# A fused graph network on one core: the mix product in three narrow passes, and gate products joined into three operations per half of the features

## The chip, the cores and the metric

The kernel runs on one core of a Trainium2 chip. The metric is the device time of one execution in microseconds (us), as the median of several runs. A core has five engines that run side by side, each with its own queue in a fixed order: TensorE (PE, the matmuls; PEld is its loading of the stationary operand), VectorE (DVE), ScalarE (ACT), GpSimd (POOL) and SyncE (SP, which here only starts DMA transfers). They wait for one another through semaphores. Matmuls accumulate into PSUM, which here is eight banks of 128 partitions x 512 float32 values; all else lies in SBUF.

## The reference, cut to what matters

64 graphs of 256 nodes with 256 features pass through two layers. The first is a gated network of three steps, each of which multiplies the features by a weight, sums them over the neighbours and updates the state with a gated recurrent cell. The second is an attention layer whose softmax weights, `alpha`, mix the projected features.

```python
def _gru_cell(inp, h, w_ih, w_hh, b_ih, b_hh):
    gi = inp @ w_ih.T + b_ih
    gh = h @ w_hh.T + b_hh
    i_r, i_z, i_n = jnp.split(gi, 3, axis=-1)
    h_r, h_z, h_n = jnp.split(gh, 3, axis=-1)
    r = jax.nn.sigmoid(i_r + h_r)
    z = jax.nn.sigmoid(i_z + h_z)
    n = jnp.tanh(i_n + r * h_n)
    return (1.0 - z) * n + z * h
...
for i in range(L):
    m = jnp.einsum('bnd,de->bne', h, weight[i])
    aggr = jnp.einsum('bst,bsd->btd', A, m)
    h = _gru_cell(aggr, h, w_ih, w_hh, b_ih, b_hh)
...
h = jnp.einsum('bnd,od->bno', x, W)
e = (h @ a_left)[:, :, None] + (h @ a_right)[:, None, :]
e = jnp.where(e > 0, e, LEAKY_SLOPE * e)
e = jnp.where(adj_matrix == 0, NEG_INF, e)
alpha = jax.nn.softmax(e, axis=-1)
return jnp.einsum('bij,bjd->bid', alpha, h)
...
h = jnp.maximum(_layernorm(x, axis=-1), 0.0)
x = x + _L0_gnn_ref(h, adj, ...)
h = jnp.maximum(_layernorm(x, axis=-1), 0.0)
x = x + _L1_gnn_ref(h, adj, ...)
```

## The kernel before, in words

**Tiling.** Two graphs form a pair, and there are 32 pairs (`NPAIR`). The state of a pair is kept transposed: two tiles `hT[db]`, one for each half of the features (`db` = 0, 1), of 128 features x 512 columns, which are the 256 nodes of both graphs. The weight of a step and the input weight of the cell are multiplied into one matrix in the set-up, so a step is a product with the adjacency (`prop`, L802) and the products of the gates (L665).

**Products in narrow passes.** Most products are not done in float32. Each operand is held three times: rounded to float32r (class `round`), the remainder of that in float16, and the value itself scaled down in float16 (class `half`). A product of two such operands is one float32r pass and two float16 passes that add into the same bank; for the weights the three parts are `fac` and the two planes of `low`. `split16` makes the three parts of an activation: `rounded` on ScalarE (L616), `remainder` on VectorE (L620 or L622), `whole_of` on ScalarE from PSUM (L627) or on VectorE from SBUF (L629). `limbs` does the first two for `prop` (L651, L652). Three products stay in float32: the turns by TensorE, the work of the last two pairs' attention, and `mix` (L953).

**Gates.** `gate` takes one bank and records one or two TensorE operations on it. For each half of the features there are five operations: r from the state (`topT`), r from the neighbours (`topF`), nh from the state, ni from the neighbours, and z from both. Each of these terms is six matmuls with 512 columns: two float32r and four float16. An operation that is `mixed` begins with the type that the operation before it ended with (`narrow`), so it holds one change of type. From the banks, ScalarE makes r (L820) and z (L833) and adds a bias to nh (L687); VectorE makes u = (r + 1) nh (L825) and adds ni (L828); ScalarE takes the tanh (L830); VectorE updates `hT[db]` with d sub, d mul and d add (L837, L839, L841).

**Attention.** Normalised features `hb[g]` of graph `g` (L738), the scores, mask and exponentials (L896, L922, L925, L927, L933) give `pm_[g]`. It is turned by a DMA transpose and two gathers, and a ScalarE copy (`join`, L710) puts the halves of each number together in `pT`. Then `mix` multiplies `hb[g]` by `pT`: four float32 matmuls with 256 columns, for each graph of a pair. Its bank is split (`c`) and multiplied by W (`project`, L964: four float32r and eight float16 matmuls of 256 columns), and L980 adds the result to the output rows. The last two pairs (`p >= NPAIR - 2`) copy the bank instead and project in float32 (L971, L975), and the last pair works in smaller pieces (L998 to L1014).

**Order.** No loop sets the order. Every operation is recorded with an engine, a cost in ns (`n`), a latency, its reads and writes and a due time, and `Plan.run` lists them: again and again it takes, over all engines, the operation that can start first by these costs; ties go by priority, which is the due time less the latency of what follows, less a hand-set number of the table `LEAD` (by name, with the prefix "first", "late" or "last" for pairs 0, 30 and 31). Operations of up to four pairs (`WINDOW`) are open at once. Buffers come from fixed sets: 28 `full`, 22 `round`, 40 `half`, 8 `bank`. The list fixes each engine's queue; on the chip the engines then only wait for semaphores. `dve2` marks VectorE operations that the plan keeps apart from GpSimd's.

Of the kernel before, what the change touches and what calls it, by code (L numbers as in the profile page):

```python
# [10 lines left out]
F32 = mybir.dt.float32  # L11
# [19 lines left out]
    "A": -111500, "A16": -23000, "G": -500, "b_nh": -3500, "b_rz": 1000, "b_rz half": 7500, "back 0": 27500,  # L31
    "back 0 gather": 88000, "back 0 of 0": 32000, "back 0 of 1": 18000, "back 1": 28500, "back 1 gather": -33000,
    "back 1 of 0": -500, "back 1 of 1": 20500, "back copy 0": -80500, "back copy 1": -5000, "c0 0": -2500,
    "c0 1": 36500, "c0 d": 32000, "c1 1": 4000, "c1 d": 7000, "d add 0": -4000, "d add 0 of 0": -16000,
    "d add 1 of 0": -44000, "d add 1 of 1": -16000, "d mul 0": 125000, "d mul 0 of 0": -18500, "d mul 0 of 1": -5500,
    "d mul 1": 89000, "d mul 1 of 0": -24000, "d mul 1 of 1": -36000, "d sub 0": -17500, "d sub 0 of 0": -3000,
    "d sub 0 of 1": -19500, "d sub 1": -9000, "d sub 1 of 0": -38000, "d sub 1 of 1": 5500, "dot 0": -136000,
    "dot 1": 3500, "exps 0": 20000, "exps 0 0": 93000, "exps 1": 1000, "exps 1 0": -65000, "exps 1 1": -11500,
    "fill": 4000, "first A": 9000, "first A16": -17000, "first back 0": -34000, "first back 1": 16000,
    "first c0 0": -23000, "first c0 1": -26500, "first c0 d": 84500, "first c1 0": -83500, "first c1 1": -28500,  # L40
    "first c1 d": -2000, "first d add 0": 7000, "first d add 1": -4000, "first d mul 0": -84500,
    "first d mul 1": -6000, "first d sub 0": -44000, "first d sub 1": 1000, "first dot 1": 17500,
    "first exps 0": 8000, "first exps 1": -4000, "first fill": 35000, "first g0 0": -7000, "first g0 1": 69000,
    "first g0 d": -1000, "first g1 0": -8000, "first g1 1": 89500, "first g1 d": -21000, "first h0 0": 46000,
    "first h0 1": -4000, "first h0 d": 38000, "first h1 0": 44000, "first h1 1": -44500, "first h1 d": 32000,
    "first hi 0": -5500, "first hi 1": 10000, "first in 0 eps": -165000, "first in 0 pow": -11500,
    "first in 0 relu": 500, "first in 0 shift": 38000, "first in 0 stats": -16500, "first in 1 eps": -17000,
    "first in 1 pow": 2000, "first in 1 relu": 17000, "first in 1 shift": -21000, "first in 1 stats": 16000,
    "first in hi 0": -78500, "first in hi 1": 8000, "first in lo 1": 44500, "first leaky 0": 48000,
    "first leaky 1": -1500, "first line 0": -10000, "first line 1": 54000, "first lo 1": 76000, "first load": -18000,  # L50
    "first mask 0": 113000, "first mask 1": 32500, "first max 0": 16500, "first max 1": 9000,
    "first mid 0 eps": -31500, "first mid 0 pow": 3500, "first mid 0 relu": -5000, "first mid 0 shift": 500,
    "first mid 0 stats": 20500, "first mid 1 eps": -15000, "first mid 1 relu": 13000, "first mid 1 shift": -15000,
    "first mid 1 stats": 6000, "first mix 1": -29000, "first nh 0 scale": 32000, "first nh 1 scale": 8500,
    "first ni 0 topF": 28500, "first out 1": 4000, "first p copy 0": -72000, "first p copy 1": -25000,
    "first p turn 0 gather": -21000, "first p turn 1": -66000, "first p turn 1 gather": -1500,
    "first project 0": 32000, "first project 1": -3000, "first prop 0": 21000, "first prop 1": -12000,
    "first r 0 topF": -55500, "first r 0 topT": -47000, "first r 1": 31500, "first r 1 topF": 16000,
    "first r 1 topT": -52000, "first recip": 14500, "first res 0": 3500, "first right 0": 26000, "first store": -3500,
    "first tanh 0": -51500, "first tanh 1": -8000, "first total": -32000, "first turn 0": -153500,  # L60
    "first turn 1": 34500, "first turn copy 0": 33500, "first u 0": 12000, "first u 1": 16000, "first u add 0": -500,
    "first u add 1": -21500, "first z 0": -24000, "first z 0 topF": -32000, "first z 1": -33000,
    "first z 1 topF": -33500, "g0 0": 108000, "g0 1": 251500, "g0 d": 500, "g1 0": 6000, "g1 d": -49000,
    "h0 0": 39500, "h0 1": 50500, "h1 0": -43000, "h1 1": 311000, "h1 d": 112000, "hi 0": 3000, "hi 1": -7000,
    "in 0 eps": 39000, "in 0 pow": -1000, "in 0 relu": -124000, "in 0 stats": -49000, "in 1 eps": 7500,
    "in 1 pow": 17000, "in 1 relu": 19000, "in 1 shift": -14500, "in 1 stats": 323500, "in hi 0": -36000,
    "in hi 1": 40000, "in lo 0": -4000, "in lo 1": 33500, "last A": 18500, "last A16": 500, "last back 0": -94000,
    "last back 0 of 0": 1000, "last back 0 of 1": -1000, "last back 1": 24000, "last back 1 of 0": -55500,
    "last d add 0": 71500, "last d add 0 of 1": 27000, "last d add 1": 13000, "last d add 1 of 0": -2000,
    "last d add 1 of 1": 25000, "last d mul 0 of 0": 19000, "last d mul 0 of 1": -8000, "last d mul 1": -149500,  # L70
    "last d mul 1 of 0": -500, "last d mul 1 of 1": 6000, "last d sub 0": -34500, "last d sub 0 of 0": 7000,
    "last d sub 0 of 1": 37000, "last d sub 1": -20000, "last d sub 1 of 0": -74500, "last d sub 1 of 1": -111000,
    "last dot 0": -74000, "last dot 1": -7500, "last exps 0 0": 3000, "last exps 0 1": 1000, "last exps 1 0": -33500,
    "last exps 1 1": 120000, "last g0 0": -2500, "last g0 1": -30000, "last g0 d": -16000, "last g1 0": -50000,
    "last g1 1": 9000, "last g1 d": -39500, "last h0 0": -23500, "last h0 1": -33500, "last h0 d": -22000,
    "last h1 0": 41500, "last h1 1": 95500, "last h1 d": 31000, "last hi 0": 25500, "last hi 1": 16000,
    "last in 0 eps": -12000, "last in 0 pow": 34000, "last in 0 shift": 98000, "last in 0 stats": -52000,
    "last in 1 eps": -8000, "last in 1 pow": 87500, "last in 1 relu": 500, "last in 1 shift": -77500,
    "last in hi 0": -16500, "last in hi 1": 65000, "last in lo 0": -8000, "last in lo 1": 16000,
    "last leaky 0": -8000, "last leaky 1": 39000, "last lo 0": 12000, "last lo 1": -89500, "last load": -72500,  # L80
    "last mask 0": 32000, "last mask 1": 90000, "last max 0": 16000, "last max 1": -8000, "last mid 0 eps": 5000,
    "last mid 0 pow": -29500, "last mid 0 shift": -4500, "last mid 0 stats": 18500, "last mid 1 pow": -85500,
    "last mid 1 relu": 80500, "last mid 1 shift": -18000, "last mid 1 stats": -8500, "last mix 0 0": -56000,
    "last mix 0 1": -29500, "last mix 1 0": -17000, "last mix 1 1": -47000, "last mix copy 0 0": -24500,
    "last mix copy 1 0": -23000, "last mix copy 1 1": 4000, "last nh 0 of 0 scale": 15000,
    "last nh 0 of 0 topF": -6000, "last nh 0 of 1 topF": -24000, "last nh 0 scale": -32000, "last nh 0 topF": -17500,
    "last nh 1 of 0 scale": 96000, "last nh 1 of 0 topF": 8000, "last nh 1 of 1 scale": -47000,
    "last nh 1 of 1 topF": -32000, "last nh 1 scale": -64000, "last ni 0 of 0 topF": -5500,
    "last ni 0 of 1 topF": -51000, "last ni 0 topF": 5500, "last ni 1 of 0 topF": 500, "last ni 1 of 1 topF": 1500,
    "last ni 1 topF": -90500, "last out 0 0": 17500, "last out 0 1": 1000, "last out 1 0": -15000,  # L90
    "last out 1 1": -91000, "last p copy 0 0": -90500, "last p copy 0 1": -63000, "last p copy 1 1": -66500,
    "last p turn 0 0": -134000, "last p turn 0 1": -25000, "last p turn 1 0": -7500, "last p turn 1 1": -21000,
    "last project 0 0": 2000, "last project 0 1": 500, "last project 1 0": 111000, "last project 1 1": -32500,
    "last prop 0": 6000, "last prop 1": 48500, "last r 0": -16000, "last r 0 of 0 topF": 22000,
    "last r 0 of 0 topT": 7000, "last r 0 of 1": -14000, "last r 0 of 1 topF": 58000, "last r 0 of 1 topT": -40500,
# [238 lines left out]
def tile_gated_gnn_then_gat(  # L334
# [45 lines left out]
    G = 2  # L380
# [678 lines left out]
```

## Time and profile before

| | us |
|---|---|
| median of 3 runs | 1970.34 (1968.96 to 1971.46) |
| the profiled execution | 1970.78 |
| its span in the profile | 1969.0 |
| TensorE busy | 1953.8 |
| VectorE busy | 1548.4 |
| ScalarE busy | 1543.8 |
| GpSimd busy | 193.7 |

The page lists busy time by engine, the span in 40 slices, the DMA queues, the chain of work that ended last, and the costliest groups of instructions. Lines such as L665 are lines of the kernel before. A matmul's busy time runs on beside the next one's, so the mean of one matmul (379 ns for 512 columns of float16) is longer than the distance between two starts. A float32 matmul appears as two records.

```profile
L665 PE MATMUL bank<-half,low_hh 128*128 128x512 f16 (+1 forms) x2328 | 613.9, 379 | 0.0
...
L732 POOL TENSOR_TENSOR small<-small,nhalf 128x2 f32<-128x2 f32 x128 | 103.8, 811 | 1456.8 <-DVE small L730 1398.3
```

The columns are line, engine, operation, output and input, shape and count, then the busy time in us and the mean of one in ns, then the engine's idle time ahead of these instructions and what ended most of it.

### The profile page before, as it was taken

The page shows a single profiled execution, that of the slowest core. Times are in us where ns is not written, and L with a number is a line of the kernel's source. Part 1 is how long each engine was busy: PE and PEld are TensorE (multiplying, and loading weights), DVE is VectorE, ACT ScalarE, POOL GpSimd, SP SyncE. Part 2 cuts the span into 40 slices and gives each one's busy share as a digit, 9 for nine tenths or more (in the row PEclk, how much of TensorE's full clock was granted, in tenths as well). Part 3 has the DMA queues.
Part 4 walks back from the last instruction along what each step waited for, and adds up shares of the span by engine and source line. Part 5 has one row for each costly group of instructions (what it writes and reads, how often), then busy time and mean ns, then how long its engine had stood idle before and what let it go on. Part 6 is the DMA issues. An engine that isn't in the chain of part 4 may idle for free.

```text
span 1969.0 us, 30480 instructions
## 1 busy us (share of the span) xinstructions
PE 1953.8 (99%) x9965; PEld 1210.8 (61%) x9965; DVE 1548.4 (79%) x3714; ACT 1543.8 (78%) x2653; POOL 193.7 (10%) x262
## 2 busy tenths in 40 slices
PE   8999999999999999999999999999999999999998
PEld 5556665666665666656666656666656666566667
DVE  7687778778788777788787787787887787887776
ACT  5577887778887778887778887788777788777865
POOL 1001011011010011010010110110100110100000
PEclk9999999999999999999999999999999999999999
DMA  4256776667776687876687776677666768656632
GB/s 122 45 101 125 134 136 115 118 122 142 145 127 110 116 138 133 140 129 112 119 137 142 134 125 109 125 139 147 125 108 120 139 132 142 129 108 125 114 75 60
DMA packets 734463, 239.36 MB, mean 122 GB/s; under 512 B 658256, under 2 KB 734304, under 8 KB 734304
## 3 DMA queue, kind: packets, MB, share of 16 engines
q1 hardware_dynamic: 734272, 237.41, 65.8%
q8 instruction: 78, 1.28, 0.3%
q14 instruction: 81, 0.66, 0.2%
q10 hardware_dynamic: 32, 0.01, 0.0%
HBM read 61.09 MB, written 16.84 MB: 40 GB/s over the span
## 4 chain that ended last, share of the span: by engine, by line
PE 97%; DVE 2%; ACT 1%; issue 0%; DMA 0%; ACTq 0%; DVEq 0%
PE bank L665 77%; PE bank L802 9%; PE bank L953 6%; PE bank L964 4%; PE bank L592 0%; PE bank L868 0%; PE bank L519 0%; PE bank L975 0%; PE bank L1006 0%; PE bank L1014 0%; DVE full L839 0%; DVE full L544 0%; ACT full L738 0%; DMA rows<-in_L_gnn_b_hh_dram 0%; DVE full L841 0%
## 5 line engine op out<-in xcount | busy, mean ns | idle before, releaser
L665 PE MATMUL bank<-half,low_hh 128*128 128x512 f16 (+1 forms) x2328 | 613.9, 379 | 0.0
L665 PE MATMUL bank<-half,low 128*128 128x512 f16 (+1 forms) x2328 | 606.0, 378 | 0.0
L665 PE MATMUL bank<-round,fac_hh 128*128 128x512 f32 (+1 forms) x1164 | 398.7, 432 | 0.0
L665 PE MATMUL bank<-round,fac 128*128 128x512 f32 (+1 forms) x1164 | 393.5, 428 | 0.0
L710 ACT COPY full<-full 128x1024 uint16<-128x1024 uint16 x304 | 349.6, 1159 | 44.7 <-DMA full<-full 38.8
L665 PEld LDWEIGHTS <-low 128*128 128x128 f16 x2328 | 214.3, 98 | 273.9 <-issue 44.4
L665 PEld LDWEIGHTS <-low_hh 128*128 128x128 f16 x2328 | 198.4, 98 | 283.3 <-issue 101.5
L665 PEld LDWEIGHTS bank<-round,fac 128*128 128x128 f32 x1164 | 214.6, 189 | 58.1
L665 PEld LDWEIGHTS bank<-round,fac_hh 128*128 128x128 f32 x1164 | 214.5, 189 | 57.0
L732 POOL TENSOR_TENSOR small<-small,nhalf 128x2 f32<-128x2 f32 x128 | 103.8, 811 | 1456.8 <-DVE small L730 1398.3
L820 ACT ACTIVATE full<-bank,b_rz 128x512 f32<-128x512 f32 (+1 forms) x194 | 131.7, 680 | 104.7 <-PE bank L665 102.3
L833 ACT ACTIVATE full<-bank,b_rz 128x512 f32<-128x512 f32 (+1 forms) x194 | 131.8, 679 | 93.8 <-PE bank L665 93.4
L620 DVE TENSOR_TENSOR half<-bank,round 128x512 f16<-128x512 f32 x192 | 132.0, 688 | 75.2 <-ACT round L616 26.6
L825 DVE SCALAR_TENSOR_TENSOR full<-full,bank 128x512 f32<-128x512 f32 (+1 forms) x194 | 131.5, 678 | 61.2 <-ACT full L820 58.9
L830 ACT ACTIVATE full<-full,vec 128x512 f32<-128x512 f32 (+1 forms) x194 | 135.1, 710 | 56.1 <-DVE full L828 56.1
L616 ACT ACTIVATE round<-bank 128x512 fp32r<-128x512 f32 x252 | 150.9, 599 | 32.6 <-PE bank L802 31.5
L839 DVE SCALAR_TENSOR_TENSOR full<-full,full 128x512 f32<-128x512 f32 (+1 forms) x194 | 132.1, 681 | 55.1 <-ACT full L833 52.4
L652 DVE SCALAR_TENSOR_TENSOR half<-full,round 128x512 f16<-128x512 f32 x184 | 125.7, 684 | 57.5 <-ACT round L651 57.5
L627 ACT ACTIVATE half<-bank 128x512 f16<-128x512 f32 x252 | 144.5, 598 | 8.7 <-DVE half L620 6.3
L687 ACT ACTIVATE bank<-bank,b_nh 128x512 f32<-128x512 f32 (+1 forms) x194 | 125.6, 648 | 25.8 <-PE bank L665 25.5
L837 DVE TENSOR_TENSOR full<-full,full 128x512 f32<-128x512 f32 (+1 forms) x194 | 141.3, 739 | 4.3 <-ACT full L830 4.2
L828 DVE TENSOR_TENSOR full<-full,bank 128x512 f32<-128x512 f32 (+1 forms) x194 | 128.4, 673 | 17.5 <-PE bank L665 14.8
(106 smaller groups left out, 2465.9 us busy)
## 6 DMA issues: line engine op xcount, KB each, us to landing
full<-full SPq DMA_DIRECT2D x484, 128.0 KB, 3.5
x<-in_x_dram SPq DMA_DIRECT2D x64, 256.0 KB, 3.4
adj<-in_adj_dram SPq DMA_DIRECT2D x64, 256.0 KB, 3.4
full<-in_x_dram SPq DMA_DIRECT2D x64, 256.0 KB, 4.2
full<-full SPq DMA_DIRECT2D x248, 64.0 KB, 2.7
out_dram<-full SPq DMA_DIRECT2D x62, 256.0 KB, 2.9
full<-line SPq DMA_DIRECT2D x62, 128.0 KB, 4.3
full<-full SPq DMA_TRANSPOSE x304, 3.6
```

Of the source, the lines that this page charges most:

```text
L616: act(name + " 0", A512 if bank else C512, lambda: nc.scalar.activation(v0.t, v.t, AF.Copy, scale=up), r=[(v, ALL)], w=[(v0, ONE)])
L620: rem = lambda: nc.vector.tensor_sub(v1.t, v.t, v0.t.bitcast(F32))
L627: act(name + " d", A512, lambda: nc.scalar.activation(vd.t, v.t, AF.Copy, scale=up * C), r=[(v, ALL)], w=[(vd, ONE)])
L665: return [(j, lambda start, j=j, kb=kb: nc.tensor.matmul(bank.t[:, cols], fs(j, kb), s[kb][j].t[:, cols], start=start, stop=True, skip_gro ...
L710: act(name, 1065, lambda: nc.scalar.copy(dst.t.bitcast(U16).rearrange("p (j n b) -> p j n b", j=2, b=2), src.t.bitcast(U16).rearrange(f"p ...
L802: nc.tensor.matmul(pa.t[:, ts(g, N)], b, m[:, ts(sb, N)], start=(n == 0), stop=True, skip_group_check=True)
L820: act(f"r {db}{of}", fit(575, part), lambda b=r_, k=pr, db=db, cols=cols: nc.scalar.activation(b.t[:, cols], k.t[:, cols], AF.Tanh, bias=b ...
L825: dve(f"u {db}{of}", fit(S512, part), lambda u=u, k=ph, b=r_, cols=cols: nc.vector.scalar_tensor_tensor(u.t[:, cols], b.t[:, cols], 1.0, k ...
L830: act(f"tanh {db}{of}", fit(615, part), lambda u=u, en=en, cols=cols: nc.scalar.activation(u.t[:, cols], u.t[:, cols], AF.Tanh, bias=b_i[: ...
L833: act(f"z {db}{of}", fit(575, part), lambda b=z_, k=pz, db=db, cols=cols: nc.scalar.activation(b.t[:, cols], k.t[:, cols], AF.Tanh, bias=b ...
L837: dve2(f"d sub {db}{of}", fit(V512, part), lambda u=u, d=d, cols=cols: nc.vector.tensor_sub(d.t[:, cols], d.t[:, cols], u.t[:, cols]), r=[ ...
L839: dve2(f"d mul {db}{of}", fit(V512, part), lambda d=d, b=z_, cols=cols: nc.vector.scalar_tensor_tensor(d.t[:, cols], b.t[:, cols], 1.0, d. ...
```

## The change

Mix: for all but the last two pairs the two operands are split like the others. `m` are the parts of `hb[g]` (ScalarE `m 0`, VectorE `m 1` and `m d`), `p` those of `pT` (ScalarE `p 0`, VectorE `p 1` and `p d`), and `mix` is four float32r and eight float16 matmuls with 256 columns in place of four float32 ones. Gates: `products` replaces `passes` and `gate`. An operation now takes jobs on several banks, and does one type over all of them before the next type. For each half of the features there are three operations: r and nh from the state; r and ni from the neighbours; z from both. The bias of nh is added right after the first. The planned costs of some operations and the whole table `LEAD` have other values (they move the order alone), and the buffers of an operation are kept in the order in which they are named.

```diff
-    A512, V512, S512, VP256, C512 = 475, 605, 660, 392, 522
+    A512, V512, S512, VP256, C512 = 477, 603, 603, 392, 521
...
+    UP_H, UP_P = 2.0**11, 2.0**14
...
-    def gate(name, e, terms, tops, apart=False, bias=None, part=ALL):
...
+    def products(name, jobs, tops, part):
+
         cols, cost, cost16 = columns(part), PASS if len(part) == 2 else PROP, PASS16 if len(part) == 2 else PROP16
...
+        n = sum(len(terms) for _, _, terms, _ in jobs)
+
+        def go():
+            fs = lambda m, j, kb, e: fac[m][:, kb, ts(e, P)] if j == 0 else low[m][:, j - 1, kb, ts(e, P)]
+            new = {id(bank) for bank, _, _, first in jobs if first}
+            for j in (1, 2, 0) if narrow[0] else (0, 1, 2):
+                for bank, e, terms, _ in jobs:
+                    for m, s, kb in [(m, s, kb) for m, s in terms for kb in range(DB)]:
+                        nc.tensor.matmul(bank.t[:, cols], fs(m, j, kb, e), s[kb][j].t[:, cols], start=id(bank) in new, stop=True,
+                                         skip_group_check=True)
+                        new.discard(id(bank))
...
-                    pr = gate(f"r {db}{of}", db, [("hh", hs), (i, gs)], tops, True, part=part)
+                    en = 2 * DB + db
+                    pr, ph, pn, pz = (Buf("bank") for _ in range(4))
+                    own, near = ("hh", hs), (i, gs)
+                    products(f"r {db}{of} topT", [(pr, db, [own], True), (ph, en, [own], True)], tops, part)
+                    act(f"nh {db}{of} scale", fit(575, part), lambda k=ph, db=db, cols=cols: nc.scalar.activation(
+                        k.t[:, cols], k.t[:, cols], AF.Identity, bias=b_nh[:, db : db + 1]), r=[("b_nh", ONE)], w=[(ph, ONE)])
+                    products(f"r {db}{of} topF", [(pr, db, [near], False), (pn, en, [near], True)], tops, part)
...
-                    ph = gate(f"nh {db}{of}", en, [("hh", hs)], tops, bias=b_nh[:, db : db + 1], part=part)
...
-                    pn = gate(f"ni {db}{of}", en, [(i, gs)], tops, part=part)
...
-                    pz = gate(f"z {db}{of}", DB + db, [("hh", hs), (i, gs)], tops, part=part)
+                    products(f"z {db}{of} topF", [(pz, DB + db, [own, near], True)], tops, part)
...
-        dve(name + " stats", 1000, stats, r=[(src, ALL)], w=[(sm, (0, 1))])
+        dve(name + " stats", 880, stats, r=[(src, ALL)], w=[(sm, (0, 1))])
...
-                act(f"leaky {g}", 365, lambda b=sc[g], nb=nb, pR=pR, sm=sm, pr=pr: nc.scalar.activation(
+                act(f"leaky {g}", 415, lambda b=sc[g], nb=nb, pR=pR, sm=sm, pr=pr: nc.scalar.activation(
...
+            turned = lambda b: b.t.rearrange("p (i j n) -> p i j n", j=NB, n=P)
             if p < NPAIR - 2:
+                m0, m1, m2 = Buf("round"), Buf("half"), Buf("half")
+                act(f"m{g} 0", C512, lambda b=m0, v=hb[g]: nc.scalar.activation(b.t, v.t, AF.Copy, scale=UP_H), r=[(hb[g], ALL)], w=[(m0, ONE)])
+                dve2(f"m{g} 1", V512, lambda b=m1, v=hb[g], t=m0: nc.vector.scalar_tensor_tensor(
+                    b.t, v.t, UP_H, t.t.bitcast(F32), op0=ALU.mult, op1=ALU.subtract), r=[(hb[g], ALL), (m0, ONE)], w=[(m1, ONE)])
+                dve2(f"m{g} d", 340, lambda b=m2, t=m0: nc.vector.tensor_copy(b.t, t.t.bitcast(F32)), r=[(m0, ONE)], w=[(m2, ONE)])
+                ps = split16(f"p{g}", pT, UP_P, part=1.0)
+
+                def mix(ms=(m0, m2, m1), ps=ps, pg=pg, turned=turned):
+                    js = (1, 2, 0) if narrow[0] else (0, 1, 2)
+                    for n, (j, db, jb) in enumerate((j, db, jb) for j in js for db in range(DB) for jb in range(NB)):
+                        nc.tensor.matmul(pg.t[:, ts(db, N)], parts(ms[j])[:, jb, ts(db, P)], turned(ps[j])[:, :, jb, :],
+                                         start=(n == 0), stop=True, skip_group_check=True)
+
+                pe(f"mix {g}", 4 * (PROP + 2 * PROP16), mix, mixed=True, r=[(b, ALL) for b in ps] + [(b, ONE) for b in (m0, m1, m2)], w=[(pg, ONE)])
```

## The prediction

> **What bounds the kernel now.** I read the head of the page first, then who waited for whom on TensorE, then the chain that ended last, then the time order of a steady pair.
>
> ```profile
> span 1969.0 us, 30480 instructions
> ...
> PE 1953.8 (99%) x9965; PEld 1210.8 (61%) x9965; DVE 1548.4 (79%) x3714; ACT 1543.8 (78%) x2653; POOL 193.7 (10%) x262
> ...
> PEclk9999999999999999999999999999999999999999
> ```
>
> TensorE is busy 99% of the span at full clock. What it lacks is 15.2 us, and the waits of its queue name most of it:
>
> ```profile
> PE bank L495 <- DMA rows<-in_L_gnn_b_hh_dram: 4.9, 1, 4.9
> PE bank L868 <- DVE full L841: 3.6, 3, 1.8
> PE bank L853 <- DVE full L841: 2.3, 2, 1.8
> PE bank L868 <- DVE small L734: 0.6, 1, 0.6
> PE bank L975 <- ACT full L971: 0.3, 1, 0.3
> PE bank L802 <- DVE half L652: 0.2, 1, 0.2
> ```
>
> These are the first load, two places near the end, and 0.2 us of all the rest. The chain of waits, in order of time, repeats itself:
>
> ```profile
> 1014.33 29.42 PE bank L665 x132
> 1045.59 10.70 PE bank L665 x48
> 1057.19 5.34 PE bank L665 x24
> 1074.13 29.42 PE bank L665 x132
> ```
>
> One pair of graphs takes 59.80 us, 97% of the chain is TensorE, and between 237 and 1732 us no TensorE instruction waits for anything. So a steady pair lasts as long as its matmuls, and a nanosecond taken off them comes off the time, if the other engines keep up. Their room, in the busy times of that stretch (PE, PEld, DVE, ACT, POOL):
>
> ```profile
> 237.02:1731.85 1494.83, 1494.83 (x7602) 917.66 (x7601) 1193.98 (x2852) 1207.08 (x2053) 154.51 (x200) 1.00 0.71 128
> ```
>
> It is 25 pairs, so a pair holds 47.8 us of VectorE and 48.3 us of ScalarE in 59.8.
>
> A rule speaks against this reading. The Trainium skill, "Perfetto Trace Analysis", section "Identifying the Most-Contended Engine", says that matmul busy time is a bad measure and that weight-load busy time is to be read instead; that is 61% here, which would leave TensorE slack and make this change worth nothing (1970 us). The starts below decide against it.
>
> **The change, part by part.** Matmul prices are distances between starts in time order, since busy times overlap:
>
> ```profile
> 1021.76 0.59 PE L665 MATMUL bank<-half,low 128*128 128x512 f16 x2
> 1022.19 0.59 PE L665 MATMUL bank<-half,low_hh 128*128 128x512 f16 x2
> ...
> 1063.28 3.62 PE L953 MATMUL bank<-full,full 128*128 128x256 f32 x16
> 1066.55 0.82 PE L665 MATMUL bank<-round,fac_hh 128*128 128x512 f32 x2
> ...
> 1070.34 1.04 PE L964 MATMUL bank<-low_W,half 128*128 128x256 f16 x8
> 1071.13 0.72 PE L964 MATMUL bank<-fac_W,round 128*128 128x256 f32 x4
> 1071.70 0.63 PE L802 MATMUL bank<-round,round 128*128 128x256 f32 x4
> ```
>
> (1) Mix. A float32 matmul of 256 columns is two records of 216 ns (medians of the starts in the steady stretch; the same starts give 109 ns for a float16 matmul of 256 columns, 118 for float32r, and 216 and 233 for 512). A mix is 4 of them, 8 records, 1.73 us. The new one is 4 float32r and 8 float16 matmuls of 256 columns. That is the shape of a project (L964), which takes 1070.34 to 1071.70, 1.36 us with its change of type; from the medians 4 x 118 + 8 x 109 = 1.344 us. It applies to 30 of 32 pairs, 60 mixes: 60 x (1.728 - 1.344) = **-23.0 us**. What the trace of before lacks is float16 and float32r with a moving operand read as two blocks of 128 columns. The float32 mix reads it just so, and its 216 is twice 108, the pace of one block; I take no penalty. The bounds: all 12 at the cheapest row, 109, is 60 x 1.308 (2.2 us better); all 12 at 121, the dearest start distance of a 256-column matmul outside float32 (L802), is 60 x 1.452 (6.5 us worse).
>
> (2) Joined gate products. The same 36 matmuls per half of the features, with 3 changes of type instead of 5. In the order of instructions I counted changes from float32r to float16: 615 before, 449 after; back: 607 and 445. A float32r matmul followed by the first float16 takes 464 ns up to the next start where 233 + 216 = 449 is due, so 15 ns; the way back takes 451, 2 ns. 166 x 15 + 162 x 2 = **-2.8 us**. Bounds: 0 and, at twice that, -5.6.
>
> (3) Added splits. On ScalarE 120 (m 0, p 0), on VectorE 120 remainders (m 1, p 1) and 120 casts (m d, p d); the instruction counts show no other, and no DMA more or less. Their nearest rows, by starts:
>
> ```profile
> 1028.91 0.42 DVE L629 TENSOR_SCALAR half<-full 128x512 f16<-128x512 f32 x1
> 1029.25 1.28 DVE L622 SCALAR_TENSOR_TENSOR half<-full,round 128x512 f16<-128x512 f32 x2
> ...
> 1041.84 0.68 DVE L652 SCALAR_TENSOR_TENSOR half<-full,round 128x512 f16<-128x512 f32 x1
> 1042.44 0.68 DVE L927 TENSOR_REDUCE small<-full 128x2 f32<-128x512 f32 x1
> ```
>
> A remainder holds VectorE 0.60 us, a cast 0.34; a rounding from SBUF (L616, L651) holds ScalarE about 0.52. Per pair that is 4 x 0.94 = 3.8 us of VectorE and 2.1 of ScalarE: 51.5 and 50.4 us in a pair of 58.9 (87% and 86%, from 80 and 81). The cover is TensorE's 58.9 us; I price them at **0**. With no cover at all 113 + 62 us would come on top, which is the far bound and no likely one: the added work would have to stand on the path 60 times over. A finer look: laying the order of all engines' instructions beside TensorE's, in stretches of 10 us of matmuls between 800 and 1040, VectorE is never given over 1.10 of a stretch (before: 1.03) and rarely under 0.65 (before: down to 0.42). The new work fills the hollows.
>
> (4) New waits. A mix used to wait for one ScalarE copy (p copy, L710); it now waits for p 1 on VectorE behind p 0 behind that copy. In the order, p 1 stands right in front of its mix in about a fifth of its reads. Behind p 1 on VectorE stand mostly lo (for the next prop), u (for the gate) and the remainder of a g or c, so lateness there would reach TensorE again at once. But before, L651 in front of prop and L710 in front of mix stood as close, in 75 and 24 reads, and cost 0.2 us in all. r's tanh may start only after 24 matmuls instead of 12, 2.7 us later. What is late next is the update of h, its turn and split, and the next layer's prop. In the order at least 16.4 us of matmuls lie between the last z product and the first prop that needs it (18.2 before); the way takes about 11.6: z 0.68, two operations of 0.68, turn 3.6 and gather 3.5 by DMA, join 1.16, hi 0.62, lo 0.68. Covered, so 0.
>
> The second rule that speaks against: the Trainium skill's "GPSIMD Engine Reference", section "1. Specifications", has GpSimd share its SBUF interfaces with VectorE, contended when VectorE reads two SBUF inputs, as every m 1 and p 1 does. The row is GpSimd's pow (L732): 710 ns median, 1293 longest, of 128. Were all at the longest, GpSimd would work 75 us more of its 1775 idle; no TensorE wait names it, so 0 by the trace.
>
> (5) New leads order set-up and end anew. TensorE's idle 15.2 us is all there is to gain, and 4.9 of it is the first load; about 5 us either way, 0 taken.
>
> Sum, against the profiled execution: 1970.8 (span 1969.0, 1.8 around it) - 23.0 - 2.8 = 1945.0; the span would be 1943.2. The median of the three runs lies 0.4 below that execution. I say 1945; a period of 58.9 us instead of 59.8.
>
> **The rivals.**
> First, mixes wait for p 1: about 24 of 60 find one VectorE instruction (0.60 us) too many ahead. 24 x 0.60 = 14.4 us back, 1960. For it: VectorE at 87%, and the tight places. Against: tight places cost nothing before.
> Second, and slower: the way from gates to the next prop becomes the bound. r is 2.7 us later, and five queued ACT and DVE steps each lose time on fuller engines. If the 4.8 us of slack are gone and 2.66 us come through once a pair, 32 x 2.66 = 85 us: 1945 + 85 = 2030. It turns the sign once it costs over 25.8 / 32 = 0.81 us a pair. Against: the slack above, and matmuls of other pairs between.
> Third, the joined products don't save their switches: 1948.
>
> A measurement of this kernel tells 0.2% (3.9 us) from no change.
>
> **How the numbers follow.** Forecast 0.72, its own range 1938 to 1953 (mix at its bounds, 5 us at the ends). Waits at the mix 0.13, around 1960; recurrence 0.09, 2030; no switches saved 0.06. The range 1938 to 1960 leaves out the recurrence, half of the waits and a few per cent below. Faster: 0.72 + 0.06 + nearly all of 0.13 gives 0.88; within 0.2%, a stronger case of the waits, 0.03; slower 0.09.
>
> **What would show it.** Mix as 12 matmuls in 1.34 to 1.36 us; TensorE busy about 1928 us, still 99%; a period of 58.9; VectorE near 87% and ScalarE near 86% in the steady stretch; no TensorE wait on p 1 beyond a few us. Wrong if TensorE's waits in that stretch pass 5 us, if a mix takes over 1.45 us, or if starts at a change of type lie as before but as many remain.

## The result and the profile after

| | median, us | lowest to highest | runs | ratio to before, 95% interval |
|---|---|---|---|---|
| before | 1972.02 | 1968.67 to 1975.67 | 12 | 1 |
| changed | 1971.38 | 1965.03 to 1974.87 | 12 | 0.9992 (0.998 to 1.0004) |

The change makes no difference that this measurement can tell. 1945 was forecast, with 1938 to 1960 around it. The head of the profile page of the changed kernel (from here on lines are those of the changed kernel, unless another is named):

```profile
span 1969.9 us, 31220 instructions
...
PE 1938.0 (98%) x10205; PEld 1226.0 (62%) x10205; DVE 1667.7 (85%) x3954; ACT 1599.2 (81%) x2773; POOL 193.1 (10%) x262
...
PEclk9999999999999999999999999999999999999999
```

TensorE has 16 us less to do by its busy time, at the same clock, and the span is as long as before. VectorE has 119 us more work and ScalarE 55 us more, about what was foretold (113 and 62). So the gain was made and lost again. The busy times of the steady stretch (PE, PEld, DVE, ACT, POOL) say where:

```profile
237.02:1731.85 1494.83, 1481.38 (x7777) 929.50 (x7776) 1292.87 (x3046) 1248.43 (x2146) 147.99 (x198) 1.00 0.73 128
```

Before, TensorE was busy for all of these 1494.83 us; now 13.5 us are missing. TensorE's waits between 237 and 1732 us name them (total us, times, longest); in the kernel before this view had no entry:

```profile
PE bank L969 <- DVE half L617: 5.0, 12, 0.6
PE bank L668 <- DVE half L615: 3.9, 12, 0.3
PE bank L950 <- DVE half L617: 3.9, 4, 1.6
PE bank L969 <- ACT round L611: 0.2, 1, 0.2
```

L969 is project, L668 a gate product, L950 the mix; L617 and L615 are the remainders (c 1, p 1; g 1). The parts of a split are named 0 (rounded), 1 (remainder) and d (whole); g is the split of prop's bank, h that of the state, c that of the mix's bank. All three products wait for the operand of their first float16 pass. In start distances the loss is larger, since idle time counts only from the end of the matmul ahead, which lies past the point where the next one usually starts (for 256 columns of float16 273 ns busy, 109 ns between starts): what matmuls start later than usual for their type, where over 0.1 us, sums to 19.8 us in the stretch, the steady loss of the tables below (project 7.7, gate product after a project 5.9, mix 5.6). A pair takes 59.85 us by the first instructions of successive pairs; without those 0.79 us it would be 59.06, where 58.94 was forecast.

The matmuls cost what was expected. A mix in time order:

```profile
1028.11 0.63 PE L950 MATMUL bank<-round,round 128*128 128x256 f32 x4
1028.59 1.05 PE L950 MATMUL bank<-half,half 128*128 128x256 f16 x8
1029.47 1.89 PE L668 MATMUL bank<-half,low_hh 128*128 128x512 f16 x8
```

1028.11 to 1029.47 is 1.36 us. The chain that ended last is where the picture changed. By engine it was 97% TensorE before; now:

```profile
PE 74%; ACT 11%; DMA 5%; DVE 5%; issue 2%; SPq 2%; POOL 0%; ACTq 0%; DVEq 0%
```

Between 237 and 1732 us it leaves TensorE 17 times for more than 3 us; it comes back at a gate product 8 times, at a project 6 times and at a mix 3 times. 11 of these ways pass a p d of 0.83 us, and 14 a DMA transfer of the turns. Here is one that has no transfer (start, us, what):

```profile
1043.66 8.05 PE bank L668 x36
1051.71 0.02 issue
1051.73 0.04 ACT bank L807
...
1061.94 0.62 ACT round L646
1062.56 1.07 ACT full L695
1063.63 0.02 issue
1063.65 0.83 DVE half L624
1064.48 0.60 DVE half L615
1065.08 0.02 issue
1065.11 0.60 ACT half L622
...
1069.21 0.50 ACT half L622
1069.71 0.02 issue
1069.73 0.53 DVE half L617
...
1070.34 0.49 DVE full L985 x2
1070.83 0.29 issue
1071.13 0.69 DVE half L615
1071.82 0.04 issue
1071.86 1.24 PE bank L668 x5
```

Read it from the top. A gate product ends and lets ScalarE scale its bank (L807). From there ScalarE works its queue off almost without a gap for some 18 us (the lines left out are its joins, tanh, roundings). A join (L695, p copy) releases p d on VectorE (L624, a split that the change added), behind which stands the remainder g 1 (L615). ScalarE's g d (L622) reads the same bank and is listed behind g 1, so it waits for it; more ScalarE work; c 1 (L617), two outputs (L985), another g 1, and only then the next gate product. This way starts and ends on TensorE, and from its end TensorE's own queue leads to the next one: that is what I call the loop. Mixes lie on it in part only: of the 68 us of mixes in the steady stretch (50 of 1.36) the chain holds 32. While a way through the other engines is longer than TensorE's work beside it, matmuls beside it can be taken away without a gain.

A late remainder need not mean that VectorE is behind. At 10 of the 16 places in the steady stretch where project's first float16 matmul starts late, VectorE had stood idle for 1.73 us until ScalarE's c d was done, which reads the same bank and is listed in front of c 1. One of them, ScalarE first, then VectorE, then TensorE:

```profile
1189.39 0.65 ACT L611 ACTIVATE round<-bank 128x512 fp32r<-128x512 f32 x1
1189.87 0.67 ACT L622 ACTIVATE half<-bank 128x512 f16<-128x512 f32 x1
1190.57 0.69 DVE L617 SCALAR_TENSOR_TENSOR half<-bank,round 128x512 f16<-128x512 f32 x1 [1.73 <-ACT half L622]
1191.31 0.94 PE L969 MATMUL bank<-low_W,half 128*128 128x256 f16 x7 [0.48 <-DVE half L617]
```

### The profile page after: what moved, and what is told of

It is laid out like the page before. It is cut to its first block, busy times and chain, and to the rows that moved or that the text cites. A ratio compares the mean times of both kernels' runs of the same rounds, so it can differ in the third digit from the quotient of the medians.

```text
span 1969.9 us, 31220 instructions
## 1 busy us (share of the span) xinstructions
PE 1938.0 (98%) x10205; PEld 1226.0 (62%) x10205; DVE 1667.7 (85%) x3954; ACT 1599.2 (81%) x2773; POOL 193.1 (10%) x262
## 4 chain that ended last, share of the span: by engine, by line
PE 74%; ACT 11%; DMA 5%; DVE 5%; issue 2%; SPq 2%; POOL 0%; ACTq 0%; DVEq 0%
PE bank L668 62%; PE bank L787 5%; DMA full<-full 5%; ACT full L695 2%; PE bank L969 2%; PE bank L950 2%; ACT half L622 2%; ACT round L611 2%; ACT full L723 1%; SPq L687 1%; ACT round L646 1%; DVE half L615 1%; DVE half L617 1%; PE bank L587 1%; DVE half L624 1%
## 5 line engine op out<-in xcount | busy, mean ns | idle before, releaser
L668 PE MATMUL bank<-half,low_hh 128*128 128x512 f16 (+1 forms) x2328 | 596.4, 379 | 0.0
L668 PE MATMUL bank<-half,low 128*128 128x512 f16 (+1 forms) x2328 | 590.0, 377 | 4.3 <-DVE half L615 4.3
L668 PEld LDWEIGHTS <-low 128*128 128x128 f16 x2328 | 226.1, 98 | 267.4 <-issue 11.5
L695 ACT COPY full<-full 128x1024 uint16<-128x1024 uint16 x304 | 352.5, 1168 | 41.4 <-DMA full<-full 33.7
L668 PEld LDWEIGHTS <-low_hh 128*128 128x128 f16 x2328 | 208.5, 98 | 271.4 <-issue 69.1
L668 PE MATMUL bank<-round,fac 128*128 128x512 f32 (+1 forms) x1164 | 365.2, 422 | 0.0
L668 PE MATMUL bank<-round,fac_hh 128*128 128x512 f32 (+1 forms) x1164 | 361.1, 418 | 0.0
L717 POOL TENSOR_TENSOR small<-small,nhalf 128x2 f32<-128x2 f32 x128 | 107.9, 843 | 1570.0 <-DVE small L715 1482.5
L668 PEld LDWEIGHTS bank<-round,fac 128*128 128x128 f32 x1164 | 217.8, 188 | 63.2
L668 PEld LDWEIGHTS bank<-round,fac_hh 128*128 128x128 f32 x1164 | 214.4, 189 | 54.4 <-issue 0.3
L807 ACT ACTIVATE bank<-bank,b_nh 128x512 f32<-128x512 f32 (+1 forms) x194 | 126.8, 653 | 102.2 <-PE bank L668 101.4
L617 DVE SCALAR_TENSOR_TENSOR half<-full,round 128x512 f16<-128x512 f32 x252 | 180.8, 723 | 10.4 <-ACT round L611 9.3
L825 DVE TENSOR_TENSOR full<-full,full 128x512 f32<-128x512 f32 (+1 forms) x194 | 132.6, 683 | 46.8 <-ACT full L818 43.9
L622 ACT ACTIVATE half<-bank 128x512 f16<-128x512 f32 x252 | 149.1, 607 | 9.3 <-DVE half L615 6.2
L611 ACT ACTIVATE round<-full 128x512 fp32r<-128x512 f32 x252 | 154.0, 625 | 2.0 <-DVE full L829 1.9
L615 DVE TENSOR_TENSOR half<-bank,round 128x512 f16<-128x512 f32 x192 | 131.2, 685 | 25.8 <-ACT half L622 20.6
```

Source lines behind the costliest of these rows:

```text
L611: act(name + " 0", A512 if bank else C512, lambda: nc.scalar.activation(v0.t, v.t, AF.Copy, scale=up), r=[(v, ALL)], w=[(v0, ONE)])
L615: rem = lambda: nc.vector.tensor_sub(v1.t, v.t, v0.t.bitcast(F32))
L617: rem = lambda: nc.vector.scalar_tensor_tensor(v1.t, v.t, up, v0.t.bitcast(F32), op0=ALU.mult, op1=ALU.subtract)
L622: act(name + " d", A512, lambda: nc.scalar.activation(vd.t, v.t, AF.Copy, scale=up), r=[(v, ALL)], w=[(vd, ONE)])
L668: nc.tensor.matmul(bank.t[:, cols], fs(m, j, kb, e), s[kb][j].t[:, cols], start=id(bank) in new, stop=True, skip_group_check=True)
L695: act(name, 1065, lambda: nc.scalar.copy(dst.t.bitcast(U16).rearrange("p (j n b) -> p j n b", j=2, b=2), src.t.bitcast(U16).rearrange(f"p ...
```

## The experiments

All edits but one (e14) leave the order of the operations on every engine as it is; within a product on TensorE e5 and the runs built on it change the order of the passes. Each was timed beside the kernel before on the same chip; comparisons go by ratios to that.

**Added work taken off VectorE and GpSimd (e1 to e4).** GpSimd's cast of the adjacency (L741) on 2 of 512 columns, prop reading the upper halves of the float32r copy instead; then m 1 and m d, then p 1 and p d, then all four on 2 columns, which leaves old data in the rest of the split. Of each line the changed call alone is shown; p d is narrowed like p 1.

```diff
-nc.gpsimd.tensor_copy(A16[g].t.bitcast(BF16), A[g].t.bitcast(F32))
+nc.gpsimd.tensor_copy(A16[g].t.bitcast(BF16)[:, :2], A[g].t.bitcast(F32)[:, :2])
...
-b.t, v.t, UP_H, t.t.bitcast(F32), op0=ALU.mult, op1=ALU.subtract)
+b.t[:, :2], v.t[:, :2], UP_H, t.t.bitcast(F32)[:, :2], op0=ALU.mult, op1=ALU.subtract)
...
-rem = lambda: nc.vector.scalar_tensor_tensor(v1.t, v.t, up, v0.t.bitcast(F32), op0=ALU.mult, op1=ALU.subtract)
+rem = lambda k=2 if name[0] == "p" else GN: nc.vector.scalar_tensor_tensor(v1.t[:, :k], v.t[:, :k], up, v0.t.bitcast(F32)[:, :k], op0=ALU.mult, op1=ALU.subtract)
```

> The changed kernel in its own order, but GpSimd's cast of the adjacency (L741) is done on two columns only, and prop reads the upper halves of the float32r adjacency in its place, which hold the same numbers. Theory of the collision (GpSimd's cast holds a VectorE split for 0.4 us, 40 times in the profile, and TensorE waits for what stands behind): TensorE's waits in the steady stretch fall from about 25 us to 10, time 1955 to 1960. Theory of the load (VectorE is simply too full): under 3 us gained, 1968 to 1972. Theory of the gates or transfers: no change, 1971.

> The changed kernel in its own order, with m 1 and m d done on two columns only (the rest of these buffers is old data): 1.9 us of VectorE work less per pair, all of it far ahead of the mix that needs it. Load: half of the lost time or more comes back, 1950 to 1960. Collision: VectorE's queue runs ahead of the plan and the cast meets other work, unclear, 1955 to 1970. Chain (p 1 right in front of its mix): no change, 1968 to 1972.

> The changed kernel in its own order, with p 1 and p d done on two columns only: also 1.9 us of VectorE work less per pair, but on the way from p copy to mix. Load: as the kernel with m narrow, 1950 to 1960. Chain: the waits of mix (about 10 us with those of its weight loads) go and the others stay, 1960 to 1965. Gates or transfers: 1971.

> The changed kernel in its own order, with m 1, m d, p 1 and p d all on two columns: VectorE has about the work of before, TensorE's order and matmuls are those of the changed kernel. If the added splits cost the time (by load, chain or collision), 1945 to 1950, the time that the prediction gave. If the joined gates, the transfers or the new order cost it, 1965 to 1972 remains.

| run | median, us | ratio, interval | steady loss, us |
|---|---|---|---|
| changed | 1971.38 | 0.9992 (0.998 to 1.0004) | 19.8 |
| e1, no cast | 1967.81 | 0.998 (0.997 to 0.999) | 15.1 |
| e2, m narrow | 1965.31 | 0.9968 (0.9955 to 0.9981) | 12.0 |
| e3, p narrow | 1962.52 | 0.9954 (0.9939 to 0.9969) | 9.3 |
| e4, m and p narrow | 1959.09 | 0.9938 (0.9923 to 0.9953) | 8.0 |

The collision with GpSimd, my first theory, fell: it holds about 2.4 us (0.9992 to 0.998, with intervals that overlap), not most of the 26. The added VectorE work holds 10.6 us (0.9992 to 0.9938); m alone gives 4.7 and p alone 7.5, whose sum these intervals don't tell from 10.6. e3 came where the chain theory had it, e4 between its two ranges, and e2 only within the widest of its three, that of the collision. And with VectorE's work back near the old amount (1585 us busy, 1548 before) 8.0 us of steady loss stay, of which e4's waits show the gate's as the largest:

```profile
PE bank L668 <- DVE half L615: 2.1, 7, 0.3
PE bank L969 <- DVE half L617: 1.1, 4, 0.5
PE bank L950 <- DVE half L617: 0.4, 1, 0.4
PE bank L969 <- ACT round L611: 0.2, 1, 0.2
```

**The order of the passes, and a mix of one pass (e5 to e8).**

```diff
-for j in (1, 2, 0) if narrow[0] else (0, 1, 2):
+for j in (2, 1, 0) if narrow[0] else (0, 2, 1):
```

The same in mix and project. e6 adds the edit of e1, e8 those of e1 and e4. e7 keeps the old order of passes and loops over `j in (0,)` in the mix.

> Only the order of the two float16 passes in every gate product, mix and project is exchanged: the pass that needs the remainder (c 1, g 1, h 1, p 1) comes after the pass that needs the whole (c d, g d, h d, p d) instead of before it. The same matmuls, the same order on every other engine. Theory of late remainders (the steady waits of 20 us stand in front of the first float16 pass, because its remainder comes 0.5 us late): the remainder gets 0.43 us (mix, project) to 0.86 us (gates) more time, so two thirds of the waits at project, mix and gate (19 us together) go: steady waits of 5 to 9 us, 1957 to 1961 us. Rival (a chain around the loop through VectorE and ScalarE sets the period, and TensorE's waits only show where it comes due): the waits move to other places, 1968 to 1973 us.

> The exchange of the passes together with the GpSimd cast of the adjacency on two columns (prop reads the upper halves of the rounded adjacency, the same numbers). Theory of late remainders: the 3.6 us that the cast alone gave are in part the same waits, so 1 to 3 us under the run with the passes alone: 1955 to 1959 us. Rival (loop through the engines): 1965 to 1969 us.

> The mix does only its float32r pass (4 matmuls of the 12); the two float16 passes are left out, all splits stay, and the order on every engine stays. TensorE has 60 x 0.86 = 52 us less to do. Theory of late remainders (TensorE's own work still sets the period, with local waits on top): most of the 52 us shows, 1922 to 1935 us. Rival (a chain through VectorE and ScalarE sets the period): under 15 us of it show and the rest becomes TensorE's waiting, 1956 to 1970 us.

> All three suspects taken away at once: the added splits of VectorE on two columns, the GpSimd cast on two columns, and the passes exchanged. The m and p remainders and wholes hold old data beyond two columns. Theory of late remainders on a fuller VectorE: steady waits under 3 us, and the time is the forecast plus the mis-sized terms, 1948 to 1953 us. Rival (something else in the new order makes TensorE wait): steady waits stay at 6 us or more, 1955 to 1959 us.

| run | median, us | ratio, interval | steady loss, us | pair, us |
|---|---|---|---|---|
| e5, passes exchanged | 1957.34 | 0.9924 (0.9906 to 0.9942) | 5.2 | 59.29 |
| e6, and no cast | 1956.63 | 0.9928 (0.9913 to 0.9942) | 4.6 | 59.31 |
| e7, mix of one pass | 1961.97 | 0.9952 (0.9939 to 0.9965) | 57.8 | 59.72 |
| e8, all off | 1953.32 | 0.9912 (0.9897 to 0.9927) | 1.7 | 59.22 |

A pair is the time between the first instructions of successive pairs. e5 came as the theory of late remainders said, but e7 came as its rival said, and e7 is the plainer witness. 52 us of matmuls were taken off (60 x (1.344 - 4 x 0.118)), and the time fell by 8 (0.9992 to 0.9952); the rest turned into waiting, most of it here:

```profile
PE bank L969 <- DVE half L617: 18.0, 36, 0.6
PE bank L969 <- ACT round L611: 13.5, 17, 1.7
PE bank L668 <- DVE half L615: 4.0, 12, 0.3
PE bank L950 <- ACT round L611: 1.1, 3, 0.6
```

The pair hardly moved, 59.72 from 59.85. The chain of e7 has no mix in the steady stretch, and little more than half of it is TensorE's:

```profile
PE 53%; ACT 17%; DVE 12%; DMA 10%; SPq 4%; issue 3%; POOL 0%; DVEq 0%; ACTq 0%
```

Both findings fit one picture: a loop through several engines, DMA among them, sets the period, and it runs through the remainders; to use a remainder last, not second, lets TensorE go on with the other float16 pass meanwhile and shortens the loop. No run changed the transfers, so their share in it is not measured. In e5 the chain is TensorE's again:

```profile
PE 92%; DMA 2%; ACT 2%; DVE 2%; issue 1%; SPq 0%; POOL 0%; DVEq 0%; ACTq 0%
```

With e5's order the cast makes no difference that can be told (e6; the intervals lie on one another). e8 leaves 1.7 us of steady loss, as its theory had it, and 1953.32 us, 0.3 above its range: the three suspects together hold nearly all of the steady loss.

**Where the loop closes, and how near it lies (e9 to e11).** e9 puts all added splits on 2 columns on both engines (as in e4, and `activation(v0.t[:, :k], v.t[:, :k], ...)` for p 0, likewise m 0; p from pair 7 on). e10 is e5 with the mix of one pass. e11 exchanges the passes in the gate products alone.

> All added splits on two columns, on both engines: m 0, m 1, m d in all pairs and p 0, p 1, p d from pair 7 on (before that the buffers hold nothing yet); the other columns keep old data. VectorE loses some 85 to 95 us of work, ScalarE 50 to 55; matmuls and orders stay. The run that narrowed the VectorE splits alone took 1959.1. Theory of the loop (gate products, ScalarE's queue worked off without a gap for some 20 us, a remainder on VectorE, the next gate products; once in two pairs): less work in ScalarE's queue shortens the loop, TensorE's waits fall under 3 us, 1951 to 1955 us. Rival (only VectorE's lateness matters): no gain over 1959.1, 1957 to 1961 us.

> The passes exchanged and the mix cut to its float32r pass. TensorE has 52 us less to do than in the run with the passes exchanged (1957.3). Theory of the loop: the loop through ScalarE and VectorE hardly runs through the mix, and lies just under TensorE's period, so most of the 52 us turns into waiting: 1940 to 1954 us. Rival (with the passes exchanged TensorE alone is the bound, with room behind it): 1905 to 1918 us.

> The passes exchanged in the gate products alone; mix and project as in the changed kernel. Theory of the loop: it closes where a gate product waits for g 1, so this place alone gives most of the 14 us of the full exchange: 1958 to 1963 us. Rival (each place holds its own time: gate 5.9, project 7.7, mix 5.6 us): only the 5.9 us at the gates go, 1964 to 1967 us.

e9: 1955.93, 0.993 (0.9913 to 0.9946), between the two ranges; against e4 the intervals overlap, so whether ScalarE's share of the splits matters stays open. e11: 1959.08, 0.9944 (0.9929 to 0.9958): 9.5 of the 13.4 us of e5 come from the gates alone. Its steady loss is 8.7 us, where without the 5.9 of the gates 13.9 would be left, so the losses at the other places are in part an echo of those at the gates. That fits a loop that closes there. e10: 1947.15, 0.9883 (0.9868 to 0.9897): 52 us of matmuls less than e5 bring 8. So even with the passes exchanged another bound lies right behind TensorE.

**Was it there before? (e12 to e14).** e12 and e13 are edits of the kernel before: half of each mix left out, and the passes exchanged. e14 is the changed kernel with the old mix.

```diff
-                    for jb in range(NB):
+                    for jb in range(few):
```

with `few = 1` for the first 30 pairs.

> The kernel before, with half of each mix left out (2 of the 4 float32 matmuls, for the 60 mixes of the first 30 pairs); everything else and every order stays. TensorE has 60 x 0.91 = 54 us less to do. Theory of the loop, applied to the kernel before: a way through ScalarE, VectorE and the turns already lay right under TensorE's period, unseen because TensorE was back to back; 54 us less work gives 10 to 30 us, 1940 to 1960 us. Rival (the kernel before was bound by TensorE alone, with room behind it; the loop came with the change): 1914 to 1925 us.

> The kernel before with the two float16 passes exchanged in gates and projects; every other engine's order stays. TensorE hardly waits in the kernel before, so the theory that the exchange helps only by shortening the loop expects nothing here: 1968 to 1973 us. Rival (the exchange saves TensorE time by itself, for instance at its weight loads): 1958 to 1965 us.

> The changed kernel with the old float32 mix in place of the three passes and without the splits m and p; the joined gate products and the changed leads stay, the order of all work is planned anew. If the added splits closed the loop, TensorE does not wait here and only the saved type changes show, 1966 to 1971 us with under 4 us of steady waits. Rival (the joined products and the new order lengthen the loop by themselves): steady waits of 8 us or more, 1975 to 1990 us.

e12: 1953.17, 0.9908 (0.9893 to 0.9923). Of 52 us of matmuls taken off the kernel before (60 x 1.728 / 2; the 54 above are a little high), 18 show. Its waits in the steady stretch (lines of the kernel before: L965 is project, L622 c 1, L954 the mix, L710 p copy):

```profile
PE bank L965 <- DVE half L622: 16.9, 25, 0.8
PE bank L954 <- ACT full L710: 4.6, 9, 0.8
PE bank L802 <- DVE half L652: 0.5, 1, 0.5
PE bank L665 <- DVE half L620: 0.2, 1, 0.2
```

So the kernel before already had a second bound at most 18 us under TensorE's (e12 also shortens ways that pass a mix, so it may lie nearer), and no wait of TensorE showed it. e13: 1970.03, 0.9996 (0.9987 to 1.0005): the exchange is worth nothing where TensorE sets the period; it saves no TensorE time by itself. e14: 2021.24, 1.0249 (1.0232 to 1.0266). It has less work than the changed kernel on VectorE and ScalarE and is 50 us slower, beyond the range of its rival; 36 us of its steady stretch are late starts. Its order was planned anew with leads that belong to other work, so what the joined gate products do to the loop is not told apart from the order; e8 has the joined products and the order of the changed kernel, and loses 1.7 us. Without late starts a pair of e14 takes 59.80 us, as in the kernel before (59.79): the joined products save TensorE nothing that shows.

**Which of p's splits (e15, e16).** The edits of e3, one at a time.

> Of the changed kernel only the cast p d (60 times) on two columns, the rest of its columns keep old data; p 1 and everything else as it is. In the chain of the changed kernel a p d stands once in two pairs right in front of g 1, for 0.83 us instead of 0.42. Theory of the loop: this one link gives most of the 8.9 us that p 1 and p d gave together: 6 us or more, 1960 to 1965 us. Rival (p 1, which the mix waits for, is what costs): under 3 us, 1968 to 1972 us.

> The counterpart: only the remainder p 1 (60 times) on two columns, p d as it is. Theory of the loop: p 1 lies beside the loop in most cycles, at most 4 us: 1967 to 1971 us. Rival (p 1, which the mix waits for): 5 us or more, 1960 to 1966 us.

e15: 1964.37, 0.9958 (0.9944 to 0.9973). e16: 1964.68, 0.9966 (0.9952 to 0.9981). 6.7 and 5.1 us, with intervals that overlap; together (e3) 7.5. p d, which nothing waited for in the forecast, costs about as much as p 1; that fits its place in the chain, but p 1 costs more than the theory allowed it. Both stand in VectorE's queue ahead of remainders, and either gives most of what both give. I can't name one link.

The best kernel that computes the whole is e5, 0.9924: the change is worth some 13 us more once each product uses its remainder last.

## Why the prediction was wrong, point by point

**What bounds the kernel: the step that failed first.** "A nanosecond taken off them comes off the time, if the other engines keep up", with their room read from 47.8 and 48.3 us of work in a pair of 59.8. TensorE did set the period, but the step from there to a gain asks how far the next bound is, and an average of busy time doesn't say: e12 put it at most 18 us lower, near 1953. So in that order the 25.8 us were not all to be had, even with splits that cost nothing. With this step failed the two terms that the sum put at 0, the added splits (3) and the new waits (4); in their place the runs show 19.8 us of late starts in the steady stretch.

In the kernel before, ScalarE was busy 16.95 of the 18 us between 1051.7 and 1069.7, where its mean share in the steady stretch is 81%: the packed stretch was there to be seen. The busy times of that window before (PE, PEld, DVE, ACT, POOL):

```profile
1051.70:1069.70 18.00, 18.00 (x95) 11.80 (x94) 13.26 (x30) 16.95 (x29) 4.42 (x6) 1.00 1.00 188
```

The rule that I weighed and set aside, from the Trainium skill's "Perfetto Trace Analysis", section "Identifying the Most-Contended Engine" (to judge TensorE's nearness to its roofline, read weight loads and the share of peak arithmetic, not matmul busy time), gave 1970 as I read it. That is nearer than my sum, but by luck: weight loads stand at 61% before and 62% after, and the waits of TensorE in the steady stretch name parts of splits, nearly all remainders, and none a weight load. Matmul busy time did tell what set the period in the kernel before; it did not tell how near the next bound was (e12).

**(1) Mix, -23.0.** Right: 1.36 us for 12 matmuls, and no penalty for the operand read in two blocks.

**(2) Joined gate products, -2.8.** Counted right, and worth next to nothing. A float32r matmul and the first float16 one take 468 ns in the changed kernel, where 464 was read and 449 is due: 449 changes at 19 ns are 8.5 us, 615 at 15 were 9.2, so 0.7 saved. Float32r matmuls in a row now start 1.4 ns late each, 0.7 before, which over 2441 of them in the stretch gives 1.7 us back. All start distances over the usual by less than 0.1 us sum to 8.9 us in the stretch, and to 8.0 before. Hence a period without waits of 59.06 and not 58.94, 3.0 us over the 25 pairs.

**(3) Added splits, 0.** Wrong by 10.6 us on VectorE's side alone (e4), by 12.2 with both engines (e9), which these runs don't tell apart. "The new work fills the hollows" was looked up in stretches of 10 us, too coarse to see a p d of 0.83 us right in front of a g 1.

**(4) New waits, 0.** The mix's wait for p 1 came, 3.9 us in 4 waits; but project and gate products, which the change did not touch in their operands, wait as long or longer (5.2 and 3.9). "Tight places cost nothing before" took quiet for room. GpSimd, put at 0 by the trace, costs at most a few us (e1: 2.4, not told from 0). The 24 remainders (L617, two SBUF inputs) that run beside GpSimd's cast take 1.10 us instead of 0.69. The Trainium skill's "GPSIMD Engine Reference", section "1. Specifications", has such operations contend with GpSimd, and the trace agrees in kind.

**(5) Ends, 0.** Outside the steady stretch, distances over the usual by more than 0.1 us sum to 19.1 us, and to 15.0 before: 4.1 more, within the 5 allowed.

The sum with these sizes: 1945 + 3.0 + 19.8 + 4.1 = 1971.9, beside 1971.67 of the profiled execution. That it lands on the time before is chance: the runs show nothing that ties the loss to the gain.

**The rivals.** The first (mix waits, priced at 14.4 us) has the right engine, but the mix lost 5.6 us. The second (the way from the gates becomes the bound, 2030) is the right kind of thing, a way through ScalarE, VectorE and DMA beside TensorE, but with the wrong end: it was to close at prop, and no prop wait stands in the steady stretch. I gave it 9% and a price of 2.66 us a pair; what the pairs lose in late starts is 0.79, close to the 0.81 that was to turn the sign. "Wrong if TensorE's waits in that stretch pass 5 us" was the sign that came (13.0).

## What to carry to other kernels

A back-to-back engine tells what sets the period, not how far behind the next bound is. Before work is moved off it, leave some of that work out for one run and see how much of it shows; here 18 of 52 us did. Work that is added to an in-order queue with 15 to 20% of room is not free if the queue has packed stretches inside a loop: look at each packed stretch of some 20 us, and let each consumer use the operand that comes last, last.

## What the runs showed of the hardware

A VectorE operation can lose about 0.4 us to a GpSimd operation beside it; which ones do depends on the pair. Here a memset, which reads nothing, hits a cast p d (L624), which has one input, on the very link of the loop shown above. VectorE in time order, then GpSimd, then ScalarE:

```profile
1063.65 0.83 DVE L624 TENSOR_SCALAR half<-full 128x512 f16<-128x512 f32 x1 [0.29 <-ACT full L695]
1064.40 0.67 DVE L615 TENSOR_TENSOR half<-bank,round 128x512 f16<-128x512 f32 x1
```

```profile
1063.67 0.53 POOL L878 MEMSET full<- 128x512 f32 x1 [0.93 <-ACT full L695]
```

```profile
1065.11 0.60 ACT L622 ACTIVATE half<-bank 128x512 f16<-128x512 f32 x1 [0.47 <-DVE half L615]
```

p d takes 0.83 us where 0.42 is usual; this happens 14 times, 5.7 us in all, each time with p d starting 0.02 to 0.03 us before the memset. At 13 other places p d starts 0.19 us before the memset; there p d takes 0.42 us, and the memset 0.69 where 0.53 is usual. The remainders L617, with two inputs, lose nothing beside the memset (14 times, 0.69 us), but 24 of them take 1.10 us beside GpSimd's cast L741. Small scalings (L929) take 0.57 us beside that cast where 0.17 is usual, 13 times; beside the pow L717 alone nothing is slowed. All such losses sum to 21.7 us, where the kernel before has 11.6. Where they lie off the loop they cost little: e1 took 16 us of them away and got 2.4.

ScalarE's lines show something else: g d waits 0.47 us for g 1, though both only read the bank. In the built program the reader that is listed second waits for the first, whichever engine it is on; the page has both cases (idle time of the engine, and what ended most of it):

```profile
L622 ACT ACTIVATE half<-bank 128x512 f16<-128x512 f32 x252 | 149.1, 607 | 9.3 <-DVE half L615 6.2
L615 DVE TENSOR_TENSOR half<-bank,round 128x512 f16<-128x512 f32 x192 | 131.2, 685 | 25.8 <-ACT half L622 20.6
```

The plan that makes the order does not know of these waits between readers. It does keep p d and GpSimd's operations apart, but by planned times, and on the chip they meet.
